# A fused cross-attention and mixture-of-experts kernel: the shared expert's first block moves into the memory of the keys, and two of its parts go ahead of the values of the last group but one

## The chip, the cores and the metric

The kernel runs on one core of one Trainium2 chip. The metric is the device time of one execution in microseconds (us). A core has a matrix engine (TensorE, "PE" in the profile, with the loading of its weights counted apart as "PEld"), a vector engine (VectorE, "DVE"), an activation engine (ScalarE, "ACT"), a general engine (GpSimd, "POOL") and an engine that here only starts transfers (SyncE, "SP"). Each engine works through its own queue in order; engines wait for one another through semaphores. Sixteen DMA engines move data between the chip's main memory (DRAM), the on-chip memory of 128 partitions, and within the latter. All arithmetic is in float32.

## The reference

What is computed, cut to what matters (layer norms, the top-2 routing and the sizes are kept in comments):

```python
# x: 2 x 1024 x 256, ctx: 2 x 64 x 256; 8 heads of 64
lat = layernorm(x)
q = l2norm(lat_n @ Wq) * q_scale                      # 1024 queries
k, v = split(concat([ctx_n, lat_n]) @ Wkv)            # 64 + 1024 keys
attn = softmax(where(mask, 8.0 * q @ k.T, -max))
x = x + layernorm((attn @ v) @ Wo)

h = layernorm(x)
shared = (silu(h @ shared_w1) * (h @ shared_w2)) @ shared_w3      # hidden size 1024
routed = sum over 16 experts of gate * (silu(h @ w1) * (h @ w2)) @ w3   # 2 experts per token, hidden size 256
x = x + shared + routed
```

## The kernel before

**Attention.** For each of the two batches the kernel projects the queries, keys and values of 1024 tokens, then runs `attention`. Its steps `u` = 0 to 63 go over 4 groups of 256 queries (`g`), 4 pairs of heads (`j`) and the 2 tiles of 128 queries in a group (`i`). Two steps make one `w` = `u` // 2, so `w` runs from 0 to 31. A step computes scores on TensorE (L627, L633, reading `kT`, the transposed keys), maxima on VectorE (L649), exponentials on ScalarE (L663), and a blockwise transpose on VectorE (`blocks`, L673) into a buffer from `hand()`. `exchange(w)` then has SyncE start 16 transfers (L687) that finish the transpose of the probabilities from that buffer into `pT`. `values(w, half)` multiplies them with `v` on TensorE (L718, and L710 for the 64 context keys) two `w` later, in two halves, and ScalarE copies the result into `oT` (L725).

**Buffers.** `hand()` takes the next of two buffers of 128 x 4096 floats from the pool `prob`. After the attention of the second batch they hold the probabilities of `w` = 30 and `w` = 31. `kT` (128 x 4 x 1024 floats, also 4096 per partition) is last read by the scores of step 63.

**After a group.** `attended` turns a finished group into the tokens' new state: it rescales `oT` (L532 to L543), multiplies with `Wo` (L551), takes the layer norm (statistics, L562 on ScalarE, L565 and L566 on GpSimd), takes the second layer norm, and stores `h2T`, the transposed input of the experts, to DRAM from GpSimd (L594). It yields between its pieces, and the attention's loop takes one or two pieces per step.

**The shared expert.** `expert(n)` handles block `n` of 256 tokens, 8 blocks in all. It loads the block's `h2T` (`load_block`, L205, a GpSimd transfer of 256 KB), then has 8 hidden parts (L220 on TensorE: 8 recorded matmuls each; Silu L225 on ScalarE; product L226 on VectorE into `gT`) and 2 output parts (L233, then an addition into the tokens' state, L237). All of its work memory is one buffer `own` from `hand()`: `gT` in front, then twice a loaded block `hT` with a scratch `sl`. This is the buffer of `w` = 30, so the first load waits until `exchange(30)` has read it.

**The order at the seam.** The attention leaves `values(30)` and `values(31)` over (`rest()`), marked FAR ahead of `values(31, 0)`. The loop behind it writes out this TensorE order: the two halves of `values(30)`; five hidden parts of block 0; `values(31, 0)`; one hidden part; `values(31, 1)`; then one part of the shared expert beside each piece of `attended` for the last group. The order on each engine is the program's order; nothing is rearranged on the chip except weight loads. After that come the routing, the weights of the routed experts (L911, SyncE, 12 transfers of 1 MB), 36 routed tiles (L1205, L1226), and the rest of the shared blocks with the gathers of the routed results (L1281, L1288).

Of the kernel before, what the change touches and what calls it, by code (L numbers as in the profile page):

```python
# [9 lines left out]
F32 = mybir.dt.float32  # L10
# [6 lines left out]
P = 128  # L17
# [8 lines left out]
def kernel(ctx: ExitStack, tc: tile.TileContext, a: dict, out: bass.AP):  # L26
    nc = tc.nc
    x, lat = a["x"], a["ctx_1024"]
    B, S, D = x.shape
# [5 lines left out]
    NC = D // P  # L35
    NI = INNER // P
# [5 lines left out]
    NS, _, SH = a["L0_ffn_shared_w1"].shape  # L42
# [3 lines left out]
    HB = TB // 2  # L46
# [18 lines left out]
    def hand():  # L65
        return prob.tile([P, PW], F32, tag="p", name="hand")

    at = ExitStack()
# [118 lines left out]
    h2T = dram.tile([NTT * P // HB, P, NC, HB], F32, name="h2T")  # L187
# [14 lines left out]
    shared = {"parts": 0}  # L202

    def load_block(n):
        nc.gpsimd.dma_start(out=shared["hT"][n % 2], in_=h2T[n])  # L205

    def expert(n):

        sw12, sw3, gT = shared["sw12"], shared["sw3"], shared["gT"]
        if n == 0:  # L210
            load_block(0)
        hT = shared["hT"][n % 2]
        for f in range(SH // P):
            yield SHARED
            if f == 1 and n + 1 < B * S // HB:
                load_block(n + 1)
            ph = shared["hidden"](f)
            for i in range(2):
                for c in range(NC):
                    nc.tensor.matmul(  # L220
                        ph[:, i, :], sw12[:, c, i, f * P : (f + 1) * P], hT[:, c, :],
                        start=(c == 0), stop=(c == NC - 1),
                    )
            sl = shared["sl"][f % 2]
            nc.scalar.activation(sl, ph[:, 0, :], AF.Silu)  # L225
            shared["mark"] = nc.vector.tensor_tensor(out=gT[:, f, :], in0=ph[:, 1, :], in1=sl, op=ALU.mult).ins  # L226
            shared["parts"] += 1
        for i in range(HB // P):
            yield SHARED
            g = n * HB // P + i  # L230
            po = shared["out"]()
            for f in range(SH // P):
                nc.tensor.matmul(  # L233
                    po, gT[:, f, i * P : (i + 1) * P], sw3[:, f, :], start=(f == 0), stop=(f == SH // P - 1)
                )
            xt = xs[g // NT][:, g % NT, :]
            shared["mark"] = nc.vector.tensor_tensor(out=xt, in0=po, in1=xt, op=ALU.add).ins  # L237
            shared["parts"] += 2
            if "store" in shared:
                shared["store"](g)  # L240
            else:
                done.append(g)
# [15 lines left out]
    def run_one(lanes, kinds=every_kind):  # L258
        for lane in lanes:
            while lane and lane[0].kind is None:  # L260
                lane.pop(0)
            if lane and lane[0].kind in kinds:
                kind = lane[0].kind
                lane[0].run()
                return kind
        return None
# [5 lines left out]
    with at:  # L272
# [3 lines left out]
        kvp = at.enter_context(tc.tile_pool(name="kvp", bufs=1))  # L276
# [518 lines left out]
        with tc.manual_schedule(engines=ordered):  # L795
            lanes = [[], [], []]

            def is_far():
                left = [p for p in lanes[0] if p.kind is not None]
                return left and left[0].kind == FAR  # L800

            for b in range(B):
                if b == 0:
                    xhT = pw.tile([P, NC, KEYS + M], F32, name="xhT")
                    norm = Pieces(normalized(0, xhT))

                    for _ in range(2):
                        norm.run()
                        while norm.kind != TP:
                            norm.run()  # L810
                    lanes[1].append(norm)
                with tc.tile_pool(name="ps_pp", bufs=NB, space=bass.MemoryType.PSUM, reuse_waits="tile") as ps_pp:

                    pause = [0]

                    def unhurried(lanes_):

                        if pause[0]:
                            pause[0] -= 1
                            return  # L820
                        kind = run_one(lanes_, every_kind)
                        left = [p for p in lanes_[0] if p.kind is not None]
                        if kind == LITTLE or left and left[0].kind == LATER or kind == TP and left and left[0].kind == SMALL:
                            pause[0] = 2

                    def between(t):

                        while b == 0 and run_one(lanes[1:2], every_kind) and lanes[1][0].kind not in (TP, None):
                            pass
                        if b > 0 and not is_far():  # L830
                            unhurried(lanes[:1])

                    def before_v(t):

                        if b > 0 and (t >= BEHIND or not is_far()):
                            unhurried(lanes[:1])

                    kT, qT, v = projections(b, xhT, ps_pp, between, before_v)
                while run_one(lanes[1:2], every_kind):
                    pass  # L840

                def after_values():

                    if b + 1 < B:
                        following.append(pw.tile([P, NC, KEYS + M], F32, name="xhT"))
                        lanes[1].append(Pieces(normalized(b + 1, following[0])))
                        return iter(())
                    pj.close()
                    sw = ctx.enter_context(tc.tile_pool(name="sw", bufs=1, side="right", reuse_waits="tile"))
                    sw12 = sw.tile([P, NC, 2, SH], F32, name="sw12")  # L850
                    sw3 = sw.tile([P, SH // P, D], F32, name="sw3")
                    shared.update(sw12=sw12, sw3=sw3)
                    return load_shared(sw12, sw3)

                following = []
                with tc.tile_pool(name="ps_sc", bufs=1, space=bass.MemoryType.PSUM, reuse_waits="tile") as ps_sc:
                    attention(b, xhT, kT, qT, v, ps_sc, lanes, after_values)
                xhT = following[0] if following else None
                while run_one(lanes[1:2], every_kind):
                    pass  # L860
            with tc.tile_pool(name="ps_sh", bufs=1, space=bass.MemoryType.PSUM, reuse_waits="tile") as ps_sh:

                shared["hidden"] = lambda f: ps_sh.tile([P, 2, HB], F32, tag="ph", name="ph", bufs=3)
                shared["out"] = lambda: ps_sh.tile([P, D], F32, tag="po2", name="po2", bufs=2)

                own = hand()
                o = SH // P * HB
                shared["gT"] = own[:, :o].rearrange("p (f t) -> p f t", f=SH // P)
                shared["hT"], shared["sl"] = [], []
                for i in range(2):  # L870
                    shared["hT"].append(own[:, o : o + NC * HB].rearrange("p (c t) -> p c t", c=NC))
                    shared["sl"].append(own[:, o + NC * HB : o + (NC + 1) * HB])
                    o += (NC + 1) * HB
                lanes[2] += [Pieces(expert(n)) for n in range(B * S // HB)]
                for _ in range(2):
                    run_one(lanes[:1])
                while True:
                    for _ in range(5 if is_far() else 1):
                        run_one(lanes[2:])
                    kind = run_one(lanes[:1])  # L880
                    if kind == STAT:
                        kind = run_one(lanes[:1])
                    if not kind:
                        break

    with ExitStack() as ff:
# [33 lines left out]
        def small(shape, name, dtype=F32, tag=""):  # L920
            return rp.tile(shape, dtype, name=name, tag=tag or name)
# [390 lines left out]
        with tc.manual_schedule(engines=ordered - {mybir.EngineType.Pool}):  # L1312
# [4 lines left out]
            places = small([P, P], "places")  # L1317
# [7 lines left out]
            def next_shared():  # L1325

                before = shared["parts"]
                run_one(lanes[2:])
                return shared["parts"] - before

            weights, loaded = load_experts(), shared["parts"]
            while sorting[0].kind:
                parts = next_shared()
# [15 lines left out]
            while True:  # L1349
                parts = next_shared()  # L1350
# [48 lines left out]
```

## Time and profile before

| what | value |
|---|---|
| time, median of 3 runs | 823.25 us (822.33 to 830.4) |
| time of the profiled execution | 825.75 us |
| its span, first to last instruction | 824.0 us |
| mean granted TensorE clock | 0.988 of full speed |
| TensorE busy | 768.1 us, 93% of the span |
| VectorE, ScalarE, GpSimd busy | 525.2, 346.8, 233.1 us |
| scores end on TensorE (last L633, with L627 ahead of it) | 494.72 us from the span's start |
| first routed matmul (L1205) | 655.60 us |
| last matmul of the last shared block (L233) begins its run | 807.60 us |

Times inside the span are counted from its start. The rows of a timeline give start, duration, engine, line, operation, result and operands, and the number of instructions merged into the row; in square brackets stands the idle time of the engine before it and what ended that idle time. A table of stretches gives the busy time of each engine in each stretch, with the granted TensorE clock (1.00 is full speed) and the share of the DMA engines' time that was busy. The profile is that of one execution; its own time is 2.5 us above the median of the runs.

### The profile page before, as it was taken

To read this page: it belongs to the slowest core of one execution; us is meant where nothing else is said; L and a number is where in the kernel's file an instruction comes from. 1 tells how busy PE (TensorE), PEld (TensorE's weight loads), DVE (VectorE), ACT (ScalarE), POOL (GpSimd) and SP (SyncE) were. 2 spreads that over 40 slices of the span, in tenths; PEclk is the share of its full clock that TensorE was granted. 3 is DMA by queue.
4 is the path that set the end of the run, shared out by engine and by line. 5 is a ranking of instruction groups with operands and counts; after the bars stand their busy time and mean duration, and the time that the engine had idled before them with its cause. 6 is when DMAs were issued, how large, how long until landed. Compare 5 with 4: busy or idle time off the path is not lost. (4 is left out here: it accounts for less than half of the span.)

```text
span 824.0 us, 11418 instructions
## 1 busy us (share of the span) xinstructions
PE 768.1 (93%) x3728; PEld 459.4 (56%) x3728; DVE 525.2 (64%) x1143; ACT 346.8 (42%) x718; POOL 233.1 (28%) x254
## 2 busy tenths in 40 slices
PE   5898999999999999998999997998999999999995
PEld 2443444445454454344545455787889756666884
DVE  3578999898985566997898983212675322222243
ACT  2445655655754334664565563222211133333110
POOL 7561001212133590021233132023000333230454
PEclk9999999999999999999999999999999999999998
DMA  8000888778788000787988878277500132231334
GB/s 225 0 1 1 197 195 189 175 182 196 176 198 182 1 26 0 181 213 205 245 213 227 185 195 216 80 228 229 179 14 14 40 95 83 90 89 48 102 115 124
DMA packets 55182, 110.31 MB, mean 134 GB/s; under 512 B 11744, under 2 KB 33424, under 8 KB 55120
## 3 DMA queue, kind: packets, MB, share of 16 engines
q1 hardware_dynamic: 42464, 84.59, 41.4%
q0 software_dynamic: 6656, 18.65, 8.4%
q10 hardware_dynamic: 6000, 6.29, 2.2%
q8 instruction: 32, 0.52, 0.3%
q14 instruction: 30, 0.25, 0.1%
HBM read 31.37 MB, written 11.01 MB: 51 GB/s over the span
## 5 line engine op out<-in xcount | busy, mean ns | idle before, releaser
L663 ACT ACTIVATE p<-p,nm 128x1088 f32<-128x1088 f32 x128 | 153.1, 1201 | 28.6 <-DVE nm L649 28.5
L627 PE MATMUL sc<-kT,qT 64*128 64x512 f32 x512 | 143.5, 641 | 12.1 <-DVE nm L649 11.3
L673 DVE STREAM_TRANSPOSE hand<-p 128x2048 f32<-128x2048 f32 x64 | 147.7, 2308 | 5.2 <-DMA pT<-hand 4.5
L718 PE MATMUL po<-pT,v 128*64 128x256 f32 x1024 | 128.8, 395 | 6.9 <-DMA pT<-hand 6.9
L718 PEld LDWEIGHTS po<-pT,v 128*64 128x64 f32 x1024 | 71.3, 140 | 78.5 <-issue 38.6
L220 PE MATMUL ph<-hand,sw 128*128 128x256 f32 x512 | 114.0, 380 | 1.1 <-DMA hand<-h2T 0.9
L649 DVE CUSTOM_DVE_ANT_0 p<-sc,mbias,nm 128x576 f32<-128x576 f32 x128 | 99.4, 815 | 19.3 <-PE sc L633 18.9
L220 PEld LDWEIGHTS ph<-hand,sw 128*128 128x128 f32 x512 | 96.5, 190 | 15.0 <-issue 1.6
L649 DVE CUSTOM_DVE_ANT_0 p<-sc,zero 128x512 f32<-128x512 f32 x128 | 82.8, 684 | 3.5 <-PE sc L627 0.3
L226 DVE TENSOR_TENSOR hand<-ph,hand 128x256 f32<-128x256 f32 x64 | 26.8, 422 | 78.8 <-ACT hand L225 59.7
L225 ACT ACTIVATE hand<-ph 128x256 f32<-128x256 f32 x64 | 24.0, 383 | 125.8 <-PE ph L220 103.4
L627 PEld LDWEIGHTS sc<-kT,qT 64*128 64x128 f32 x512 | 39.4, 185 | 53.7 <-issue 27.6
L1205 PE MATMUL phr<-rw,xT 128*128 x144 | 67.9, 593 | 0.3 <-ACT xT L1191 0.3
L1213 DVE TENSOR_TENSOR hid<-phr,slr 128x256 f32<-128x256 f32 x36 | 15.3, 425 | 79.9 <-ACT slr L1211 76.0
L196 POOL TENSOR_TENSOR rn<-se,neghalf 128x8 f32<-128x8 f32 (+1 forms) x34 | 55.6, 1637 | 33.5 <-DVE se L195 33.2
L233 PE MATMUL po<-sw,hand 128*128 128x256 f32 x256 | 57.2, 380 | 1.1 <-DVE hand L226 1.1
L1168 POOL DMA_INDIRECT xr<-h,tok_i x36 | 34.2, 950 | 72.5 <-PE ptx L1189 53.5
L233 PEld LDWEIGHTS po<-sw,hand 128*128 128x128 f32 x256 | 48.3, 190 | 7.9 <-DVE hand L226 1.5
L395 PE MATMUL pp<-wkv_sb,xhT 128*128 128x512 f32 (+1 forms) x96 | 48.2, 630 | 0.8 <-ACT xhT L361 0.8
L405 DVE TENSOR_REDUCE ss<-hand 128x8 f32<-128x512 f32 (+1 forms) x34 | 23.3, 684 | 37.3 <-ACT hand L403 37.0
L633 PEld LDWEIGHTS sc<-kc,qT 128*128 128x128 f32 x128 | 19.0, 188 | 48.9 <-issue 48.1
L403 ACT ACTIVATE hand<-pp 128x512 f32<-128x512 f32 (+1 forms) x34 | 20.2, 595 | 41.9 <-PE pp L395 38.3
(189 smaller groups left out, 980.8 us busy)
## 6 DMA issues: line engine op xcount, KB each, us to landing
pT<-hand SPq DMA_DIRECT2D x512, 128.0 KB
rw<-in_L_ffn_routed_w_dram SPq DMA_DIRECT2D x12, 1024.0 KB
sorted_y<-y ACTq DMA_DIRECT2D x36, 128.0 KB
h<-hn POOLq DMA_DIRECT2D x16, 128.0 KB
h2T<-hT POOLq DMA_DIRECT2D x8, 256.0 KB
sw<-in_L_ffn_shared_w_dram POOLq DMA_DIRECT2D x4, 512.0 KB
hand<-h2T POOLq DMA_DIRECT2D x8, 256.0 KB
out_dram<-x SPq DMA_DIRECT2D x16, 128.0 KB
```

The costliest lines, as they stand in the source:

```text
L196: nc.gpsimd.tensor_tensor(out=o, in0=t, in1=neghalf[: o.shape[0], :n], op=ALU.pow)
L220: nc.tensor.matmul(ph[:, i, :], sw12[:, c, i, f * P : (f + 1) * P], hT[:, c, :], start=(c == 0), stop=(c == NC - 1),)
L226: shared["mark"] = nc.vector.tensor_tensor(out=gT[:, f, :], in0=ph[:, 1, :], in1=sl, op=ALU.mult).ins
L233: nc.tensor.matmul(po, gT[:, f, i * P : (i + 1) * P], sw3[:, f, :], start=(f == 0), stop=(f == SH // P - 1))
L395: nc.tensor.matmul(pp, xhT[:, c, cols], w[:, c, w0 : w0 + INNER], start=(c == 0), stop=(c == NC - 1))
L627: nc.tensor.matmul(sc[:, r * (1 + part), :], q[rows, :], kT[rows, j, half * TB : (half + 1) * TB], start=True, stop=True,)
L649: nc.vector.tensor_tensor_reduce(out=both[:, to : to + n_], in0=sc[:, o : o + n_], in1=bias, scale=-SCALE, scalar=nm[:, 0, r : r + 1] if p ...
L663: nc.scalar.activation(p, p, AF.Exp, bias=nm[:, 1, r : r + 1], scale=-1.0, accum_out=state["sums", g][:, i, j, r : r + 1],)
L673: nc.vector.transpose(state["blocks", u // TG][:, :, 2 * i : 2 * i + 2, :].rearrange("p k r e -> p r k e"), state["p", u].rearrange("p (r ...
L718: nc.tensor.matmul(po[r * DH : (r + 1) * DH, :], v[:, c, h * DH : (h + 1) * DH], mine, start=(c == 0), stop=False,)
L1168: nc.gpsimd.indirect_dma_start(out=fetched[j], out_offset=None, in_=h2[:, :], in_offset=bass.IndirectOffsetOnAxis(ap=route["tokens"][:, j ...
L1205: nc.tensor.matmul(ph.rearrange("p i f -> p (i f)"), xT[j][:, c, :], w[:, c, bass.ds(es[j] * (2 * RH), 2 * RH)], start=(c == 0), stop=(c = ...
```

## The change

Block 0 of the shared expert gets its memory (`gT`, `hT`, `sl`) from a new tile of the name `kT`, that is, in the memory of the keys, and no longer from `own`. Blocks 1 to 7 keep `own`. `load_block(0)` is called before `own` is taken; the load of block 1, which was called at block 0's part 1, is called at its part 6. The order written for TensorE becomes: two hidden parts of block 0; the two halves of `values(30)`; three hidden parts; `values(31, 0)`; and on as before. The lines behind the new lines move by 12, the ones between by -1, so that L220, L565 and L718 become L219, L564 and L717.

```diff
     def load_block(n):
-        nc.gpsimd.dma_start(out=shared["hT"][n % 2], in_=h2T[n])
+        nc.gpsimd.dma_start(out=shared["at", n][1], in_=h2T[n])
...
-        sw12, sw3, gT = shared["sw12"], shared["sw3"], shared["gT"]
-        if n == 0:
-            load_block(0)
-        hT = shared["hT"][n % 2]
+        sw12, sw3 = shared["sw12"], shared["sw3"]
+        gT, hT, sls = shared["at", n]
         for f in range(SH // P):
             yield SHARED
-            if f == 1 and n + 1 < B * S // HB:
+
+            if f == (6 if n == 0 else 1) and n + 1 < B * S // HB:
                 load_block(n + 1)
...
-            sl = shared["sl"][f % 2]
+            sl = sls[f % 2]
...
+                keys = kvp.tile([P, NI, S], F32, name="kT").rearrange("p j s -> p (j s)")
+
+                def places(own, n):
+                    o = SH // P * HB
+                    gT = own[:, :o].rearrange("p (f t) -> p f t", f=SH // P)
+                    parts = []
+                    for i in range(2):
+                        parts.append((
+                            own[:, o : o + NC * HB].rearrange("p (c t) -> p c t", c=NC),
+                            own[:, o + NC * HB : o + (NC + 1) * HB],
+                        ))
+                        o += (NC + 1) * HB
+                    return gT, parts[n % 2][0], [sl for _, sl in parts]
+
+                shared["at", 0] = places(keys, 0)
+                load_block(0)
                 own = hand()
...
+                for n in range(1, B * S // HB):
+                    shared["at", n] = places(own, n)
                 lanes[2] += [Pieces(expert(n)) for n in range(B * S // HB)]
+                for _ in range(2):
+                    run_one(lanes[2:])
                 for _ in range(2):
                     run_one(lanes[:1])
                 while True:
-                    for _ in range(5 if is_far() else 1):
+                    for _ in range(3 if is_far() else 1):
                         run_one(lanes[2:])
```

In the changed program's order of instructions GpSimd has the same sequence as before: L564 and L565 (the former L565 and L566) of the third group, then the load of block 0, then the load of block 1. What differs there are the waits: the load of block 0 waits for the last scores on TensorE, and the wait for `exchange(30)` stands at the load of block 1. On ScalarE the copy of `values(30)` (L725) comes behind the first two Silus instead of ahead of all.

More of the change, by code (lines that the diff above doesn't have):

```diff
@@ L864 @@
                 shared["out"] = lambda: ps_sh.tile([P, D], F32, tag="po2", name="po2", bufs=2)
-                own = hand()
[L867 to L873, printed above, removed]
+                keys = kvp.tile([P, NI, S], F32, name="kT").rearrange("p j s -> p (j s)")
[12 more added lines that the diff above has]
+                load_block(0)
+                own = hand()
+                for n in range(1, B * S // HB):
+                    shared["at", n] = places(own, n)
                 lanes[2] += [Pieces(expert(n)) for n in range(B * S // HB)]
+                for _ in range(2):
+                    run_one(lanes[2:])
                 for _ in range(2):
```

## The prediction

> **What bounds the kernel now.** I read the page's busy times first, then the costliest groups, then TensorE's timeline at the seam between attention and shared expert, then GpSimd's and ScalarE's there, then short stretches with the clock, and last the waits of TensorE and SyncE behind the seam. The page:
>
> ```profile
> PE 768.1 (93%) x3728; PEld 459.4 (56%) x3728; DVE 525.2 (64%) x1143; ACT 346.8 (42%) x718; POOL 233.1 (28%) x254
> ...
> L718 PE MATMUL po<-pT,v 128*64 128x256 f32 x1024 | 128.8, 395 | 6.9 <-DMA pT<-hand 6.9
> ...
> L220 PE MATMUL ph<-hand,sw 128*128 128x256 f32 x512 | 114.0, 380 | 1.1 <-DMA hand<-h2T 0.9
> ```
>
> TensorE is the bound, and the two rows name all that the change can win on it: values that waited for exchanged probabilities, and the shared expert's wait for its first load. TensorE's timeline shows where they lie:
>
> ```profile
> 499.71 1.95 PE L718 MATMUL po<-pT,v 128*64 128x256 f32 x16
> 501.59 0.70 PE L710 MATMUL po<-cT,vc 128*128 128x256 f32 x2
> 505.57 5.36 PE L718 MATMUL po<-pT,v 128*64 128x256 f32 x32 [3.28 <-DMA pT<-hand]
> 510.86 0.70 PE L710 MATMUL po<-cT,vc 128*128 128x256 f32 x2
> 512.44 8.87 PE L220 MATMUL ph<-hand,sw 128*128 128x256 f32 x40 [0.88 <-DMA hand<-h2T]
> 521.24 1.95 PE L718 MATMUL po<-pT,v 128*64 128x256 f32 x16
> ```
>
> TensorE ends values(29) at 502.29, stands 3.28 us until exchange(30) has landed, does values(30) from 505.57, stands 0.88 us until block 0 has landed, and begins the shared expert at 512.44. So 10.15 us pass between 502.29 and 512.44: 4.16 of standing and 5.99 of values(30) (with its drain). The reader should see that values(30) now covers most of the wait for block 0. Why that block comes so late is on the other engines:
>
> ```profile
> 499.43 2.31 DVE L673 STREAM_TRANSPOSE hand<-p 128x2048 f32<-128x2048 f32 x1 [0.15 <-ACT p L663]
> ...
> 501.67 0.12 DVE L291 SCALAR_TENSOR_TENSOR less<-mvo,ro 128x2 f32<-128x2 f32 x1
> ...
> 502.59 1.09 ACT L562 ACTIVATE y<-y,less,ro 128x256 f32<-128x256 f32 x2
> ...
> 503.81 1.26 POOL L565 TENSOR_TENSOR y<-y,row_L_xattn_ln_o_w 128x512 f32<-128x512 f32 x1 [3.75 <-issue]
> 505.15 1.27 POOL L566 TENSOR_TENSOR x<-x,y 128x512 f32<-128x512 f32 x1
> 506.37 1.16 POOL L205 DMA_DIRECT2D hand<-h2T  x2
> ```
>
> The load is not issued when its buffer comes free. GpSimd's queue had the semaphores for it between 505.1 and 505.4, but GpSimd was in L566 until 506.42, and the two loads (blocks 0 and 1) follow that without a gap. L566 hangs on L565, L562, the small L291, and so on the last blockwise transpose of the attention.
>
> **The change, step by step.** *Lifting the buffer wait.* It was met at 505.4, ahead of the end of L566. In the changed order the load of block 0 still stands directly behind L565 and L566, none of whose inputs change. It is therefore issued at 506.4 again: gain nothing. If GpSimd had been free, the last scores (494.72) would have been its limit.
>
> *Landing.* Issued at 506.37, the load let TensorE start at 512.44: 6.0 us, beside exchange(31), whose transfers keep the DMA engines busy (shares of 0.85, 0.85 and 1.04 in the stretches from 505.5 to 512.5). Exchange(31) and the load of block 1 are issued as before, so I take the same 512.44. The other side is a load beside little: that of block 2, issued at 543.19, had all of its packets moved by 546.0, 2.8 us. That would allow a start at 509.3. The upper side: the last packets of the two loads fall into the slice 513 to 514, so 514. The Trainium skill, "DMA: Bandwidth & Descriptors", section "Anatomy of one DMA — SWDGE (gpsimd) path", gives a GpSimd transfer about 2.0 us and its bytes at 436 GB/s, for 256 KB an estimated 2.6 us; by that the start would be near 509.1 and the loss 3.2 us, while the row with exchange(31) beside it says 6.0.
>
> *Two parts ahead of values(30).* They go onto the path, with the wait for block 0 in front of them, and everything that TensorE has is queued behind: values(30), whose data are there from 505.5, can no longer cover it. TensorE stands from 502.29 to 512.44, 10.15 us, where it stood 4.16. Then it has the five parts, as before, and values(30) in addition. At full clock values(30) takes 1.88 + 2.42 = 4.30 us (values(31): first half 521.24 to 523.12, second 525.04 to 527.46). The old run took 5.99 because of the clock:
>
> ```profile
> 503.00:503.50 0.50, 0.00 (x0) 0.00 (x0) 0.00 (x0) 0.50 (x2) 0.00 (x0) 1.00 0.96 221
> ...
> 506.50:507.00 0.50, 0.50 (x6) 0.37 (x4) 0.00 (x0) 0.00 (x0) 0.50 (x2) 0.73 1.02 238
> ...
> 508.50:509.00 0.50, 0.50 (x6) 0.37 (x4) 0.00 (x0) 0.00 (x0) 0.00 (x0) 0.50 0.95 238
> ...
> 510.00:510.50 0.50, 0.50 (x6) 0.41 (x4) 0.00 (x0) 0.00 (x0) 0.00 (x0) 0.86 0.99 336
> ```
>
> (Stretch, its length, busy time of PE, PEld, DVE, ACT and POOL, the clock, the DMA share and GB/s.) The clock fell to half at about 506.75 and came back at 510.15, 3.4 us later; 5.99 - 4.30 = 1.69 is half of that. So the standing cost more than its length.
>
> *The clock at the new restart.* Steps of 3.41 us from 506.75 lie at 510.16, 513.57 and 516.98. The stretch that ended at 506.75 had 1.2 us of work and was followed by half clock; the one that ends at 513.57 would have 1.13, so I expect half clock from 512.44 to 516.98, 4.54 us, which loses 2.27. Bounds: one step (loss 1.7) and two (3.4), since the place of the steps may differ between executions; 1.7 is also what the one stall here measured. The Trainium skill, "TensorE: Matmul & The Clock Gate", section "HAM oscillation — how this bites in real kernels", warns of idle gaps above about 3.4 us only. The trace is stricter, since 3.28 us at 502.29 sufficed, and so did 2.18 us ahead of 25.60, with clock 0.50 from 26 to 28. By the page's warm-up of about 3.4 us at half clock (section "What's actually happening") the loss is an estimated 1.7 and the sum +6.0.
>
> *What else moves.* ScalarE's copy of values(30) now stands behind two Silus; values(31) waits for it because there is one `po` bank, but three parts (5.2 us) lie between; without that cover it would cost 0.4. The table load for Silu (1.28 us at 511.99) moves ahead to 503.7, into the standing. The products go into the keys' memory, free since 494.72. Block 1's load is issued at 507.0 in both. Block 2's loses a wait for TensorE, but TensorE waited for a load of h2T once only (0.9 us, block 0): nothing. SyncE's expert weights wait for the end of values(31) (527.66) and so move with it; the last of the 12 is issued at 589.0, the first use is at 655.60, so more than 50 us of cover.
>
> *The sum.* Before: 10.15 us from 502.29. After: 10.15 standing, 2.27 of clock, 4.30 of values(30) behind it, 16.72. Difference **+6.6 us**. Does it reach the end? Behind 521 the idle times of TensorE are 0.17, 1.01, 1.12, 1.69, 0.21, 0.62 and 0.30 us, each ended by GpSimd, VectorE or ScalarE work that itself hangs on TensorE. None is a transfer on its own clock, so nothing absorbs the delay. For the profiled execution 825.75 + 6.6 = 832.4; that execution is 2.5 above the median, so for the median 823.25 + 6.6 = **829.8**. Bounds: early landing 6.98 + 2.27 + 4.30 - 10.15 = +3.4; late landing (514) 11.71 + 2.27 + 4.30 - 10.15 = +8.1; landing as now with the short and the long clock loss 4.30 + 1.7 = +6.0 and 4.30 + 3.4 = +7.7.
>
> **The rivals.** *It does what it says:* the two parts fill the gap. If block 0 had landed by 502.3, two parts (3.46 us; their Silus begin 1.73 apart) would cover the 3.28, values(30) would run at full clock, and 10.15 would become 4.30: -5.85, 817.4. For it speaks that the parts fit the gap and that the buffer is free at 494.72; against it that the load would have to be issued by about 496, while L565 alone starts at 503.81. Standing and clock loss together must stay under 10.15 - 4.30 = 5.85 to break even; with 1.7 of clock that is a start at 506.4, the moment of the issue. 6 in 100.
>
> *The clock makes it a clear loss:* two steps at half clock (3.4), and the moved steps then catch the two stalls of 1.12 and 1.69 us between 562.4 and 566.0 in one step, which loses another 1.7: 4.30 + 3.4 + 1.7 = +9.4, 832.7. It decides if those 2.8 us of standing fall into one step of 3.41; for it speaks the 2.18 us stall that was enough at 25.6, against it that in the trace of before they did not lower it. With slower forms of the landing, 22 in 100.
>
> *An earlier landing,* +3.4, 826.7, because a standing TensorE or the new buffer eases the transfer: the transfers beside it are the same, 12 in 100.
>
> *The forecast,* landing as now and +6.0 to +7.7: 60 in 100.
>
> **How the numbers follow.** About 1% (8.2 us) is what a measurement of this kernel can tell from no change. The forecast and the early landing lie within it, slower; the rival that works lies within it as well, faster; above 1% slower is the clock's rival with late landings, 0.24. Faster by over 1% would need more than the 5.85 us that are there: 0.02. The rest, 0.74, is within 1%. The range 825.5 to 833.5 takes in the early landing and the clear loss, with a microsecond for the spread of the runs, and leaves out the version that works.
>
> **What would show it.** Right: in the changed kernel TensorE's timeline has one gap of some 10 us, ended by the load into `kT`, then two parts at clock 0.5, then values(30) with no wait for its exchange; GpSimd issues the load right behind L565 at about 506.4. Wrong: a load issued before 502; a gap under 7 us; clock 1.00 at the restart; values(31) or the routed part starting less than 5 us later than before.

## The result, and the profile after

The changed kernel takes 828.08 us (median of 22 runs, 825.4 to 830.66) against 823.11 us for the kernel before (22 runs beside them). The ratio is 1.0063 with a 95% interval of 1.0051 to 1.0074: slower by 5.2 us (4.2 to 6.1), clear of noise and within the 1%. The profiled execution took 826.21 us with a span of 824.4 us, the fifth shortest of the 22; it is not to be compared with the 825.75 us of the old profile by their difference alone. All ratios leave out slow executions, of which there was one, of memory_only below, at 3819 us.

The costliest groups on the page of the changed kernel have one of the two rows that the prediction shows of before (busy time, mean ns of one, then the idle time ahead and what ended it):

```profile
L717 PE MATMUL po<-pT,v 128*64 128x256 f32 x1024 | 126.2, 389 | 4.5 <-DMA pT<-hand 4.5
```

The other, for block 0 alone, stands in the full list of its groups:

```profile
L219 PE MATMUL ph<-kT,sw 128*128 128x256 f32 x64 | 16.1, 409 | 8.7 <-DMA kT<-h2T 8.7
```

The wait for exchanged probabilities has shrunk from 6.9 to 4.5 us over the whole run, as the change meant, and the wait for the load of block 0 has grown from 0.9 to 8.7. TensorE's timeline at the seam:

```profile
498.64 1.95 PE L717 MATMUL po<-pT,v 128*64 128x256 f32 x16
500.52 0.70 PE L709 MATMUL po<-cT,vc 128*128 128x256 f32 x2
509.88 5.14 PE L219 MATMUL ph<-kT,sw 128*128 128x256 f32 x16 [8.65 <-DMA kT<-h2T]
514.94 3.67 PE L717 MATMUL po<-pT,v 128*64 128x256 f32 x32
518.55 0.70 PE L709 MATMUL po<-cT,vc 128*128 128x256 f32 x2
519.08 5.34 PE L219 MATMUL ph<-kT,sw 128*128 128x256 f32 x24
524.36 1.95 PE L717 MATMUL po<-pT,v 128*64 128x256 f32 x16
```

One gap of 8.65 us, two parts that take 5.06 us (509.88 to 514.94) where the next ones take 1.73 each, then values(30) without a wait, in 4.14 us. GpSimd's timeline shows why the load is late:

```profile
502.75 1.26 POOL L564 TENSOR_TENSOR y<-y,row_L_xattn_ln_o_w 128x512 f32<-128x512 f32 x1 [3.75 <-issue]
504.09 1.26 POOL L565 TENSOR_TENSOR x<-x,y 128x512 f32<-128x512 f32 x1
505.29 0.61 POOL L205 DMA_DIRECT2D kT<-h2T  x1
505.90 0.55 POOL L205 DMA_DIRECT2D hand<-h2T  x1
```

The load is issued straight behind L565, as it was before, although the last scores (L632) ended at 493.66. Four stretches show the clock (stretch, length, busy time of PE, PEld, DVE, ACT and POOL, clock, DMA share, GB/s):

```profile
501.00:505.50 4.50, 0.22 (x2) 0.00 (x0) 0.00 (x0) 2.64 (x4) 2.67 (x3) 1.00 0.92 206
506.00:509.50 3.50, 0.00 (x0) 0.00 (x0) 0.00 (x0) 0.00 (x0) 0.45 (x1) 0.50 0.87 207
509.50:512.50 3.00, 2.62 (x6) 2.19 (x7) 0.00 (x0) 0.00 (x0) 0.00 (x0) 0.50 1.05 272
513.00:516.00 3.00, 3.00 (x20) 2.20 (x20) 0.85 (x2) 0.77 (x2) 0.00 (x0) 1.00 0.56 128
```

The clock falls to half inside the gap, at about 506, and stays there for the first 3 us of work.

### The profile page after: what moved, and what is told of

It reads as the page before. It is cut to its first block, busy times and chain, and to the rows that moved or that the text cites. A ratio compares the mean times of both kernels' runs of the same rounds, so it can differ in the third digit from the quotient of the medians.

```text
span 824.4 us, 11417 instructions
## 1 busy us (share of the span) xinstructions
PE 765.2 (93%) x3728; PEld 457.8 (56%) x3728; DVE 525.4 (64%) x1143; ACT 347.1 (42%) x718; POOL 232.9 (28%) x254
## 5 line engine op out<-in xcount | busy, mean ns | idle before, releaser
L717 PE MATMUL po<-pT,v 128*64 128x256 f32 x1024 | 126.2, 389 | 4.5 <-DMA pT<-hand 4.5
L717 PEld LDWEIGHTS po<-pT,v 128*64 128x64 f32 x1024 | 69.4, 138 | 75.6 <-issue 40.9
L219 PE MATMUL ph<-hand,sw 128*128 128x256 f32 x448 | 99.5, 380 | 0.2 <-DVE hand L225 0.2
L219 PEld LDWEIGHTS ph<-hand,sw 128*128 128x128 f32 x448 | 84.5, 190 | 11.8 <-DVE hand L225 0.6
L224 ACT ACTIVATE hand<-ph 128x256 f32<-128x256 f32 x56 | 21.2, 383 | 112.9 <-PE ph L219 88.4
L225 DVE TENSOR_TENSOR hand<-ph,hand 128x256 f32<-128x256 f32 x56 | 23.4, 422 | 51.8 <-ACT hand L224 51.7
L232 PE MATMUL po<-sw,hand 128*128 128x256 f32 x224 | 50.0, 380 | 1.1 <-DVE hand L225 1.1
L632 PEld LDWEIGHTS sc<-kc,qT 128*128 128x128 f32 x128 | 19.0, 188 | 49.2 <-issue 48.5
L232 PEld LDWEIGHTS po<-sw,hand 128*128 128x128 f32 x224 | 42.3, 190 | 7.2 <-DVE hand L225 1.5
```

The source lines that it names most:

```text
L219: nc.tensor.matmul(ph[:, i, :], sw12[:, c, i, f * P : (f + 1) * P], hT[:, c, :], start=(c == 0), stop=(c == NC - 1),)
L232: nc.tensor.matmul(po, gT[:, f, i * P : (i + 1) * P], sw3[:, f, :], start=(f == 0), stop=(f == SH // P - 1))
L717: nc.tensor.matmul(po[r * DH : (r + 1) * DH, :], v[:, c, h * DH : (h + 1) * DH], mine, start=(c == 0), stop=False,)
```

## The experiments

The theory: the load of block 0 keeps its place behind L564 and L565 on GpSimd, so putting two parts ahead of values(30) takes that work out of the wait that it covered, and the longer standing costs clock at the restart. The rivals: the new place of the memory costs by itself; the transfers are the bound, so that the order cannot matter; the clock is not a cost of its own.

**Only the memory (memory_only).** Block 0 in the keys' memory, order as before:

```diff
-                for _ in range(2):
-                    run_one(lanes[2:])
                 for _ in range(2):
                     run_one(lanes[:1])
                 while True:
-                    for _ in range(3 if is_far() else 1):
+                    for _ in range(5 if is_far() else 1):
```

> Block 0 lives in the memory of the keys as in the changed kernel, but TensorE's order is that of the kernel before: both halves of values(30), then five parts. Theory of the queue (the order put values(30) behind the wait for block 0): the time is that of before within 1 us, with a stall of about 3 us ahead of values(30) and one under 2 us ahead of the first part. Rival, the memory itself costs (waits or contention of the new place): the time stays near that of the changed kernel, about 5 us above before. Rival, the load lands earlier in the new place: first part starts under 5 us after the issue of the load although TensorE is busy.

Measured: 1.0002 of before (0.9989 to 1.0015). TensorE's timeline:

```profile
506.07 3.67 PE L717 MATMUL po<-pT,v 128*64 128x256 f32 x32 [2.60 <-DMA pT<-hand]
509.68 0.70 PE L709 MATMUL po<-cT,vc 128*128 128x256 f32 x2
511.56 8.87 PE L219 MATMUL ph<-kT,sw 128*128 128x256 f32 x40 [1.19 <-DMA kT<-h2T]
```

The place costs nothing that can be measured (about 1 us either way); the loss is in the order. Its load was issued at 507.56, so the first part followed 4.0 us later. That is under the 5 us of the second rival, but the second profiles below find the load as soon at the old place.

**The load issued early (early_load).** The order of the changed kernel, with the load moved into the attention, behind the last scores (`places` is defined further up for it, and the old call goes; neither is shown):

```diff
                 if u + 2 < n:
                     scores(u + 2, 1)
+                if b == B - 1 and u + 3 == n:
+                    keys = kvp.tile([P, NI, S], F32, name="kT").rearrange("p j s -> p (j s)")
+                    shared["at", 0] = places(keys, 0)
+                    load_block(0)
```

> The changed kernel with one thing moved: the load of block 0 is issued as soon as the last scores are done, ahead of L564 and L565 on GpSimd. Theory of the queue: issue near 494.8, landing near 500 to 502, two parts fill the gap, no long stall and no half clock; values(30) may wait some 0 to 1.5 us more, since its exchange shares the DMA engines with 256 KB more. Time 5 to 6 us under before (817 to 818), 10 to 11 under the changed kernel. Rival, the transfers are the bound and the load only trades places with exchange(30): values(30) starts 2 us or more later than its parts end, and the time is within 2 us of before.

Measured: 0.9958 of before (0.9941 to 0.9975), so 3.5 us faster, less than expected. GpSimd's timeline of this run has the load at:

```profile
494.16 0.59 POOL L205 DMA_DIRECT2D kT<-h2T  x1 [3.48 <-PE sc L638]
```

TensorE's timeline:

```profile
501.67 3.62 PE L231 MATMUL ph<-kT,sw 128*128 128x256 f32 x16
505.21 3.67 PE L729 MATMUL po<-pT,v 128*64 128x256 f32 x32
508.82 0.70 PE L721 MATMUL po<-cT,vc 128*128 128x256 f32 x2
509.35 5.34 PE L231 MATMUL ph<-kT,sw 128*128 128x256 f32 x24
516.68 1.95 PE L729 MATMUL po<-pT,v 128*64 128x256 f32 x16 [1.99 <-DMA pT<-hand]
```

The load now waits for the last scores only, both gaps ahead of values(30) and of block 0 are gone, and the two parts run at full clock. What is new is the wait at 516.68: values(31) now comes before exchange(31) has landed. That exchange is the next bound, as the table of stretches of this run shows (columns as above):

```profile
510.00:515.00 5.00, 4.70 (x22) 3.80 (x20) 0.85 (x2) 1.03 (x3) 0.00 (x0) 1.00 0.96 226
515.00:517.00 2.00, 0.32 (x4) 0.30 (x6) 0.42 (x1) 0.12 (x1) 0.00 (x0) 1.00 0.02 6
```

The DMA engines are busy to about 515, and TensorE goes on at 516.7, some 1.7 us after that.

**Early load, order as before (early_old_order).** The same early load with the order edit of memory_only.

> The early load, but both halves of values(30) ahead of the five parts, as before. Theory of the queue: the stall ahead of values(30) stays at 3 to 4.5 us with its half clock, only the 0.9 us ahead of the first part goes: 0 to 1 us under before. Rival, the early load alone is what counts and the order does not: as fast as the early load with two parts ahead, 5 us or more under before.

Measured: 0.9995 of before (0.998 to 1.0011). TensorE's timeline:

```profile
506.70 5.36 PE L729 MATMUL po<-pT,v 128*64 128x256 f32 x32 [3.01 <-DMA pT<-hand]
511.99 0.70 PE L721 MATMUL po<-cT,vc 128*128 128x256 f32 x2
512.53 8.80 PE L231 MATMUL ph<-kT,sw 128*128 128x256 f32 x40
```

Only the 0.9 us ahead of the first part went. The early load without the order brings nothing that can be measured, the order without the early load costs 5.2 us, and both together gain 3.5.

**The wait filled (after_fill).** The changed kernel with work whose result is left unread:

```diff
+                idle = ps_tp.tile([P, 4, P], F32, tag="tp", name="idle").rearrange("p c k -> p (c k)")
+                for _ in range(9):
+                    nc.tensor.matmul(idle, ident, v.rearrange("p t f -> p (t f)")[:, :TB], start=True, stop=True)
                 for _ in range(2):
                     run_one(lanes[2:])
```

> The changed kernel with nine matmuls of 128x512 whose result nobody reads, 7.7 us at full clock, written for TensorE between values(29) and the two parts, so that the wait for block 0 is mostly not idle. Clock as a term of the sum: half clock at the restart goes, time 1.5 to 2.3 us under the changed kernel, two parts take 3.5 us instead of 5.1. Rival, the clock is no cost of its own (two parts are slow at the start for another reason, such as the transfers beside them): time and the length of the two parts stay as in the changed kernel, or the time grows if the extra matmuls outlast the wait.

Measured: 1.0035 of before (1.0019 to 1.0051), against 1.0063 (1.0051 to 1.0074) for the changed kernel: 2.3 us less; the two intervals leave some 1.6 us of doubt either way. TensorE's timeline:

```profile
500.61 7.89 PE L887 MATMUL idle<-v,ident 128*128 128x512 f32 x18
508.88 3.69 PE L219 MATMUL ph<-kT,sw 128*128 128x256 f32 x16 [0.38 <-DMA kT<-h2T]
512.50 3.67 PE L717 MATMUL po<-pT,v 128*64 128x256 f32 x32
```

The two parts take 3.62 us instead of 5.06, though the DMA engines are as busy beside them (a share of 1.04, against 0.98 in the changed kernel). So the clock is a cost of its own; useless work at the right place buys it back.

**The same fill in the kernel before (before_fill).** Three such matmuls ahead of values(30).

> The kernel before with three matmuls of 128x512 whose result nobody reads, 2.6 us at full clock, between values(29) and values(30), so that the wait for exchange(30) is mostly not idle. values(30) should run at full clock (4.3 us instead of 6.0). If the landing of block 0 is the next limit there, the stall ahead of the first part grows by what values(30) saves, and the time falls by at most 1 us; if the clock alone were the limit, it falls by 1.7 us.

Measured: 1.0001 of before (0.9987 to 1.0016): no change. In the trace values(30) runs at full clock, and the wait for block 0 is still there:

```profile
502.74 3.67 PE L718 MATMUL po<-pT,v 128*64 128x256 f32 x32
506.34 0.70 PE L710 MATMUL po<-cT,vc 128*128 128x256 f32 x2
507.65 8.87 PE L220 MATMUL ph<-hand,sw 128*128 128x256 f32 x40 [0.61 <-DMA hand<-h2T]
```

The stall did not grow from 0.88 as expected, because the load landed 3.5 us after its issue at 504.18, not 6.0. That called for second profiles of both kernels.

**Second profiles (before_again, after_again).** Both kernels unchanged.

> The kernel before, unchanged, for a second look at the landing of block 0. If 6.0 us from issue to the first part was the place or the two loads into one buffer, it is 5.5 to 6.5 again; if it was chance, it is nearer to the 4.0 to 4.6 of the changed kernel and of the run with only the memory changed.

> The changed kernel, unchanged, for a second look at the landing of block 0 and at the clock behind it: 4.0 to 4.6 us from issue to the first part if the place decides, anything up to 6 if chance does; two parts in 4.3 to 6.9 us, depending on where the clock's stretch of 3.4 us ends.

The kernel before took 826.29 us in this one run. Its timeline:

```profile
504.55 3.67 PE L718 MATMUL po<-pT,v 128*64 128x256 f32 x32 [2.61 <-DMA pT<-hand]
508.15 0.70 PE L710 MATMUL po<-cT,vc 128*128 128x256 f32 x2
509.67 8.87 PE L220 MATMUL ph<-hand,sw 128*128 128x256 f32 x40 [0.82 <-DMA hand<-h2T]
```

With the issue at 506.02 that is 3.65 us, and values(30) ran at full clock this time. The changed kernel (828.98 us) again showed one gap, with 3.73 us from issue (505.57) to first part and 5.18 us for the two parts:

```profile
509.30 5.25 PE L219 MATMUL ph<-kT,sw 128*128 128x256 f32 x16 [7.79 <-DMA kT<-h2T]
514.48 3.67 PE L717 MATMUL po<-pT,v 128*64 128x256 f32 x32
```

So the 6.0 us and the half clock of values(30) in the profile of before belong to that execution and not to the kernel: the eight other profiles with a late load gave 3.5 to 4.1 us at the old place and 3.7 to 4.6 at the new, and of five profiles with values(30) behind its own wait two had half clock. Why the one landing took 6.0 us is open; what decides on the clock is worked out in the last section.

**A fourth part ahead of values(31) (early_four, early_four_again).** In early_load, the 3 in the loop becomes 4.

> The early load with two parts ahead of values(30) and four instead of three between it and values(31). In the run with three, TensorE stood 1.99 us for exchange(31) ahead of values(31). If that stall is all that kept the early load from its 5 to 6 us, a fourth part (1.73 us) covers it: 1.5 to 2 us under the early load with three, 5 to 5.5 under before. Rival, the executions of the two merely fell on different half-clock stretches elsewhere: no change of the median beyond 0.7 us, though the stall is gone from the trace.

> The early load with four parts once more, for a narrower interval, beside the two kernels that have the shift by one part without the early load: 5 to 8 us under before again. If the shift explains more than half of that, the theory that the early load is the cure is too strong.

Measured: 0.9918 of before (0.9898 to 0.9938), 6.8 us faster, more than expected, and again 0.9925 (0.9901 to 0.9949), 6.2 us. TensorE's timeline of the first:

```profile
505.14 3.62 PE L231 MATMUL ph<-kT,sw 128*128 128x256 f32 x16
508.68 3.67 PE L729 MATMUL po<-pT,v 128*64 128x256 f32 x32
512.29 0.70 PE L721 MATMUL po<-cT,vc 128*128 128x256 f32 x2
512.82 7.07 PE L231 MATMUL ph<-kT,sw 128*128 128x256 f32 x32
519.82 1.95 PE L729 MATMUL po<-pT,v 128*64 128x256 f32 x16
```

No wait is left at the seam (0.18 us in the second). This version beats both kernels.

**The shift by one part alone (before_six, after_four).** The fourth part also moves every later part by one against the pieces of `attended`, and the trace of early_four has 1.22 us of standing near 564 where the others have 1.12 and 1.69 in a row. So the kernel before with 6 for 5, and the changed kernel with 4 for 3:

> The kernel before with six instead of five parts between values(30) and values(31), nothing else. The early load with four parts also shifts every later part by one against the pieces of attended, and its trace lacks the 1.1 us stall near 560 and has 1.2 instead of 1.7 us in the next. If that shift is worth something by itself, this kernel is 1 to 3 us under before; if the early load and its filled gap are all, it equals before within 0.7 us.

> The changed kernel with four instead of three parts between values(30) and values(31): the same shift by one part, with the late load left in. Whatever the shift is worth should show here as well (0 to 3 us under the changed kernel); the long stall ahead of the first part stays at 7.5 to 10 us, so it should still be 2 us or more above before.

Measured: before_six 0.9981 of before (0.9966 to 0.9997), 1.6 us faster; after_four 1.0067 (1.0044 to 1.009), no gain over 1.0063. TensorE in after_four:

```profile
510.72 6.21 PE L219 MATMUL ph<-kT,sw 128*128 128x256 f32 x16 [8.30 <-DMA kT<-h2T]
516.85 3.67 PE L717 MATMUL po<-pT,v 128*64 128x256 f32 x32
```

The traces of all three kernels with the shift have stalls of 1.22 or 1.23 and 0.93 or 0.94 us where the others have 1.12, 1.69, 0.21 and 0.62, some 1.5 us less standing, which fits the 1.6. So about 1.6 of the 6.2 to 6.8 us are the shift's rather than the early load's. Why it does not show in the time of after_four is open: its interval just about allows it, and its two parts took 6.13 us in the profile, longer half clock than in the other two of this order.

## Why the prediction was right, and where its terms were off

The forecast of +6.6 us, 829.8, stands against +5.2, 828.08; sign, place and mechanism were those that it gave. The 6.6 lies a little outside the interval of 4.2 to 6.1.

*Lifting the buffer wait gains nothing:* right. The load was issued behind L565 in the changed kernel (505.29, with everything up to there about 1.1 us sooner in that execution), and early_load shows that the position in GpSimd's queue was what held it.

*Landing, 6.0 us:* mis-sized. Measured in the changed kernel 4.59, 3.73 and, in after_four, 4.23; the value had come from the one execution in which it was slow. The gap was therefore 8.65, 7.79 and 8.30 us, not 10.15. The same landing stands on both sides of the sum, so the error cancels, and what the forecast comes to is 4.30 and 2.27, values(30) and the clock. The two early starts are 0.1 us late by their own terms: 506.37 and 2.8 or 2.6 are 509.2 and 509.0. The 2.6 us estimated from the Trainium skill's "DMA: Bandwidth & Descriptors", section "Anatomy of one DMA — SWDGE (gpsimd) path", was met by no profile with exchange(31) beside the load; the shortest was 3.5.

*values(30) uncovered, 4.30 us:* right, 4.14 in the trace, and memory_only shows that the loss is in this order.

*The clock at the restart, 2.27 us:* 1.60, 1.72 and 2.67 in three profiles (5.06, 5.18 and 6.13 us less 3.46), and 2.3 by after_fill. What the prediction did not see is that the half clock of values(30) in the kernel before, which it treated as given, comes in part of the executions only; its sum does not hang on this, because block 0 landed later still there. The Trainium skill, "TensorE: Matmul & The Clock Gate", section "What's actually happening", says that the window which decides this runs free of the program. The profiles agree with that: the same stall early in the program met half clock in five executions and full clock in seven, by its place on a grid of 3.41 us (last section).

*The sum:* from the end of values(29) to the start of values(31), without its five parts of 8.80 us, the changed kernel took 14.34 and 13.59 us; after_four, with one part of 1.73 taken off, 15.04. The order of before took 10.15 (the profile), 7.73 (before_again), 8.10 (memory_only) and 8.16 (before_six, likewise corrected). The means, 14.3 and 8.5, differ by 5.8, against 16.72 and 10.15 forecast, 6.6. The small rest to 5.2 lies inside the interval. That none of it is absorbed as far as the routed part holds: the stalls up to there are the same, 1.02, 1.12, 1.69, 0.21, 0.62 and 0.30 us, save one of 0.17 that is gone, and the way from values(31) to the first routed matmul is 134.31 us against 134.36 of before.

*The signs:* one that the prediction named for being wrong did come out between the two profiles. values(31) starts 3.1 us later than before (524.36 against 521.24) and the first routed matmul as well (658.67 against 655.60), where it asked for 5. That mark had been set by the one execution of before with the slow landing. Against before_again values(31) starts 5.9 us later (518.47) and the routed part 4.2 (654.52), because that execution lost 1.7 us in between to half clock from 564.29 to 567.70.

*The rivals:* the version that works was priced at -5.85 on the condition of an early issue. With that condition met it gave -3.5, because it had not been asked what would be late next: exchange(31). With a fourth part for cover it gave more than 6, the shift of 1.6 included; by the sum above the seam takes 6.05 us in early_load and 3.99 and 4.24 in the two profiles of early_four, 2.5 and 4.4 us under the 8.5 of before. The earlier landing happened, but on both sides. The clear loss by the clock did not happen: no execution reached 832.7 (the longest took 830.66, one of before 830.4). Its condition, half clock behind the stalls of 1.12 and 1.69 us, is met in five of the traces, of before_again and before_fill as of memory_only, early_load and after_fill, but in neither of the changed kernel.

## What to carry to other kernels

Before freeing a buffer sooner, look at what stands ahead of the transfer in the queue that issues it: here the buffer had never been the last thing waited for. Work that covers a wait must not be put behind it; to fill a gap with other work, first make sure that this work's own data are there by then, and then see which transfer is late next. Two changes that are worth nothing or cost something alone (early load, order) can be a gain together, so try them in one kernel as well as apart.

## What the runs showed of the hardware

The time of one execution goes with the granted clock. Of the 22 runs of the changed kernel, the five at a mean clock of 0.989 took 825.4 to 826.59 us, and the five at 0.983 to 0.984 took 829.77 to 830.66; the correlation of time and clock is -0.95, with 0.78 us for each 0.001. A stretch of 3.4 us at half clock in which TensorE works costs 1.7 us, so a spread of 5 us between runs of the same program would be some three such stretches more or less.

Where a program stands for 2 to 3 us, the same standing was followed by half clock in one execution and not in another. Ahead of about 25.6 us twelve of the 13 traces have the same stall of 2.17 or 2.18 us; half clock followed in five of them and full clock in seven. The traces show what decides. Inside the program every stretch at half clock lasts 3.41, 6.83 or 10.24 us, one, two or three steps, and in one execution all of them begin on one grid of such steps: in before at 25.45, 168.81, 380.43 and 506.73, which are 42, 62 and 37 steps apart. What counts is how much of the standing falls into one step of that grid. The step around the wait for exchange(30) and the next one, first in before, then in before_again (columns as above):

```profile
503.31:506.73 3.42, 1.16 (x12) 0.97 (x14) 0.00 (x0) 0.37 (x1) 2.84 (x3) 1.00 0.93 210
506.73:510.14 3.41, 3.41 (x20) 2.38 (x18) 0.00 (x0) 0.00 (x0) 0.80 (x2) 0.50 0.84 202
502.85:506.26 3.41, 1.71 (x16) 1.44 (x18) 0.00 (x0) 0.48 (x1) 2.72 (x3) 1.00 0.93 207
506.26:509.68 3.42, 2.60 (x22) 1.55 (x17) 0.00 (x0) 0.78 (x2) 0.93 (x2) 1.00 0.84 243
```

In before 2.26 us of the first step are standing (3.42 less 1.16), and half clock follows; in before_again 1.70, and it does not. The other profiles of this wait agree: 3.01 us with half clock (early_old_order), 1.76 and 1.45 without (memory_only, before_six). So does the stall at 25.6: 2.02 to 2.17 us of it lie in one step in the five with half clock, at most 1.65 in the seven without. Behind the first 15 us of all 13 traces, no step at full clock with under 1.5 us of standing was followed by half clock and every one with over 1.85 was; in between both occurred. So one profile does tell the price of such a stall for its own execution, but another execution has its grid elsewhere.
